# Where a layer-norm, lightning-attention and router kernel makes its second pair's token blocks and its softmax exponentials: from the heads stage to the v stage

## The chip, the cores and the metric

The kernel runs on one core of one Trainium2 chip. Times are device microseconds (us) of one execution, from its launch to its end; the number given for a kernel is the median of several executions. The kernel before takes 1105.56 us (median of 3, 1104.92 to 1107.88). A profile is one execution taken by the hardware profiler; its span runs from the first to the last instruction.

## The reference

The input `x` has 4 sequences of 512 tokens with 512 features, in float32. The core of what is computed:

```python
xn = layernorm(x)
# attention: the 4x512 tokens, 16 heads of 128, blocks of tokens with a decay
qkv = silu(einsum('bnf,of->bno', xn, w_qkv))            # q, k, v per head
o_inter = einsum(qi * q_decay, kv)                      # state of the blocks before
o_intra = einsum(einsum(qi, ki) * diag_decay, vi)       # inside a block
kv = block_decay * kv + einsum(ki * k_decay, vi)
out = norm_w * out * rsqrt(mean(out * out) + 1e-6)      # over all heads of a token
gate = sigmoid(einsum('bnf,of->bno', xn, w_gate))
s = einsum('bno,fo->bnf', gate * out, w_out)
# router
scores = softmax(xn @ router_weight.T + router_bias)    # 64 experts
topk_w, topk_idx = top_k(scores, 8)
g = silu(xn * sum(topk_w) + einsum(topk_w, expert_bias[topk_idx]))
return x + s * g
```

## The kernel before, in words

**Tiling.** The 4 sequences are two pairs (`PB` = 2); a sequence is `NT` = 4 tiles of 128 tokens, and 512 features are `FC` = 4 chunks of 128, in two halves of `KC` = 2. A product in float32 is made of three matmuls on operands that are split into a high part in the format fp32r and the rest (`PASSES`, L27). The high part is a cast by ScalarE (`split_hi`, L99), the low part a subtraction by VectorE or GpSimd (`split_lo`, L102).

**Seven products for eight.** The two sequences of a pair and the two halves of the features make a 2x2 block matrix of tokens; two groups of output features and the two halves make one of weights. `unit` (L495) multiplies them with seven block products (`PRODUCTS`, L39) in place of eight. The token blocks are B11, B21, B22 and four sums T1 to T4 (`token_sums`, L265), the weight blocks A11, A12, A22 and four sums S1 to S4. Each product is 6 matmuls of 128x128 by 128x512. `unit` puts them in 3 of the 4 banks of the PSUM pool `ps_mm`; VectorE adds the banks together (`add`, L503, row L504). After product number i, `unit` runs the functions in `after[i]`: these are the side steps in which all other work of the kernel is placed. `plain_unit` (L536) is the same with eight plain products.

**What sets the order.** The order is written by hand. Every engine works through its own instructions in the order in which the program issues them, and waits at the first whose input or buffer is not ready. Nearly all DMAs are issued by one engine, SyncE (SP), in program order too. A pool's buffer is used again when its last reader is done.

**The stages,** with their starts in the profiled execution:

1. *Start* (0 to 14.2 us). Loads; 24 transposes of the identity that keep TensorE busy (`warm_up(WARM)`, L146); the decay masks of the 16 heads, made by ScalarE and GpSimd and stored (`make_decays`, L168, `mask_decays`, L174); layer norm of the first tiles (`layer_norms`, L225: statistics on VectorE, and `rstd` by a power on GpSimd, one instruction for each sequence; `normalise_x`, L239); transposes of the tile (`transpose`, L246, into `xf`); its blocks (`plain`, L291, or with token sums `combine`, L277); the router's logits (`logits`, L328).
2. *v* (14.2 to 201.2 us): 16 units (loop at L926). The blocks of a tile have 128 columns in a slot that both pairs share in turn (`blocks[1, n] = blocks[0, n]`, L898). Units 0 to 3 are pair 0's tiles and units 4 to 7 pair 1's, with the first half of v's weights (`ws[0]`); while unit k runs, the side steps prepare tile k+1. Units 8 to 11 are pair 1's tiles again and 12 to 15 pair 0's, with the second half (`ws[1]`, loaded in unit 4, L945, its sums in units 4 to 7, L949). Since pair 1's blocks have then overwritten pair 0's, these are made again during units 9 to 12 from `xf`, which `turn` had stored in DRAM and `load_xf` (L295) loads. Four results of a unit go through tiles of `vout` (3 buffers, L877) to DRAM (`v_unit`, L587).
3. *Heads*: 24 units for pair 0 (from 201.2 us) and 24 for pair 1 (from 556.3 us), in the loop at L1004: a gate unit for two heads, then one qk unit for each. The attention of a head runs in the side steps of the unit behind its qk unit (`attention`, L732): `scores_qk`, `states` and `attend` for both sequences, and the second sequence's `attend` in step 0 of one unit later still. Scores, states and transposes use the pool `ps_sc` (3 PSUM banks), both outputs the one bank of `ps_o` (L712), which VectorE (`y`, L721) and ScalarE (`sq`, L728) read.
   Two more things run beside pair 0's heads. `rebuild` (L300, called at L1020) makes pair 1's blocks again from stored `xf`: in units 3, 7, 11 and 15, for one tile each, VectorE makes 4 token sums and 7 low parts and ScalarE 7 casts, and each block is stored to `blocks_d` (28 stores). At pair 0's end `load_block` (L201) loads them. `routing` (L345) runs one step after each product from unit 3 on: it loads the stored logits (`load`), takes the maximum and subtracts it (`top`, `less`), applies exponentials on ScalarE (`exps`), sums and divides (`total`, `norm`), takes the best 8 (`best_of`) and writes the weights' high and low parts transposed to DRAM (`turn`, with a bank of `ps_sc`).
4. *Output projection* (903.6 us to the end; `o_head`, L810, `finish`, L803), with the router's sums (`ffn`, L767).

Two of these orders, the attention of a head and the products of a unit on one tile, are these lines:

```python
now = [
    [], f(scores_qk, b1), f(scores_qk, b0), f(states, b1), f(states, b0), f(attend, b1), [],
]
return now, f(attend, b0)
...
return blocks[p, xn][:, xi, c, bass.ts(t, P)], w.of[wn][:, wi, bass.ts(c, VW)]   # v
return w.of[wn][:, wi, bass.ts(c, P)], blocks[p, xn][:, xi, c]                   # heads
```

Of the kernel before, what the change touches and what calls it, by code (L numbers as in the profile page):

```python
# [14 lines left out]
P = 128  # L15
# [7 lines left out]
WARM = 24  # L23
# [27 lines left out]
def kernel(  # L51
# [50 lines left out]
    def split_lo(eng, lo, src, hi):  # L102
# [22 lines left out]
    xf_d = {  # L125
        (p, t): dram.tile([P, PB, FC, P], F32, tag=f"xf{p}_{t}", name=f"xfd_{p}_{t}")
        for p in range(B // PB) for t in range(NT)
    }
# [3 lines left out]
        n: dram.tile([P, 2, KC, N], F32, tag=f"b{n}", name=f"bd_{n}") for _, n, _, _ in PRODUCTS  # L132
# [52 lines left out]
    rstd = [const.tile([P, NT], F32, tag=f"rstd{b}", name=f"rstd{b}") for b in range(B)]  # L185
# [11 lines left out]
    def block(p, i, xpool, slot):  # L197
        n = XN[i]
        blocks[p, n] = xpool.tile([P, 2, KC, N], F32R, tag=f"x{slot}", name=f"blk_{n}_{p}")
# [25 lines left out]
    def layer_norms(bs, t):  # L225
        var = small.tile([P, len(bs)], F32, tag="lnvar", name=f"lnv_{bs[0]}_{t}")
        for i, b in enumerate(bs):
# [4 lines left out]
                var[:, i : i + 1], stats[b][:, t, 1:2], 1.0, LN_EPS, ALU.mult, ALU.add  # L232
            )
        for i, b in enumerate(bs):
            nc.gpsimd.tensor_tensor(
                rstd[b][:, t : t + 1], var[:, i : i + 1], mhalf[:, 0:1], ALU.pow
            )
# [20 lines left out]
    def split_blocks(p, t, eng, srcs):  # L258
        for n, src in srcs:
            blk = blocks[p, n][:, :, :, bass.ts(t, P)]  # L260
            split_hi(blk[:, 0], src)
            split_lo(eng, blk[:, 1], src, blk[:, 0])
# [32 lines left out]
    def load_xf(stage, p, t):  # L295
        xfs[p, t] = stage.tile([P, PB, FC, P], F32, tag="xf", name=f"xf_again_{p}_{t}", bufs=2)
        nc.sync.dma_start(out=xfs[p, t], in_=xf_d[p, t])


    def rebuild(stage, p, t):  # L300
        def first():
            s = stage.tile([P, 4, KC, P], F32, tag="ts", name=f"ts_{p}_{t}_r", bufs=1)
            made.extend(token_sums(nc.vector, xfs[p, t], s))

        def lo(n, w):
            split_lo(nc.vector, w[:, 1], made[1][n], w[:, 0])
            nc.sync.dma_start(out=blocks_d[n][:, :, :, bass.ts(t, P)], in_=w.bitcast(F32))

        def step(i):
            if i == 0:  # L310
                first()
            if i > 0:
                lo(*done[-1])
            if i == len(XN):
                return
            n = XN[i]
            subs, src = made
            for f in {0: subs[0:2], 2: subs[2:4]}.get(i, ()):
                f()
            w = stage.tile([P, 2, KC, P], F32R, tag="piece", name=f"piece_{n}_{p}_{t}", bufs=3)  # L320
            split_hi(w[:, 0], src[n])
            done.append((n, w))

        made, done = [], []
        return [lambda i=i: step(i) for i in range(len(XN) + 1)]


    def logits(stage, p, t):  # L328
# [11 lines left out]
        if t == NT - 1:  # L340
            for j in range(PB):
                nc.sync.dma_start(out=scores_d[p * PB + j], in_=scores[p][:, j])


    def routing(stage):  # L345
# [7 lines left out]

        def top(b):
            den[b] = small.tile([P, NT], F32, tag="top", name=f"top_{b}")
            nc.vector.reduce_max(den[b], sc[b], axis=AX.X)

        def less(b):
            nc.vector.tensor_tensor(sc[b], sc[b], full(den[b]), ALU.subtract)

        def exps():
            for b in range(B):
                nc.scalar.activation(sc[b], sc[b], AF.Exp)
# [41 lines left out]
        for b in range(B):  # L405
            out += [lambda b=b: top(b), lambda b=b: less(b)]
# [498 lines left out]
    for i in range(2):  # L905
        ds[i] = make_decays(ds[i], hs[i])
# [257 lines left out]
```

## Time and profile before

| | us |
|---|---|
| median of 3 executions | 1105.56 (1104.92 to 1107.88) |
| the profiled execution, its time | 1105.03 |
| the profiled execution, its span | 1103.3 |
| mean granted TensorE clock | 0.992 of full |

| stretch of the span (us) | length | TensorE busy | VectorE | ScalarE | GpSimd | granted clock | DMA share |
|---|---|---|---|---|---|---|---|
| 0 to 20 (start) | 20 | 15.7 | 9.9 | 14.6 | 9.8 | 0.74 | 0.84 |
| 20 to 140 (v, tiles prepared) | 120 | 111.7 | 91.5 | 58.9 | 98.6 | 1.00 | 0.48 |
| 140 to 200 (v, rest) | 60 | 60.0 | 40.8 | 26.2 | 33.4 | 1.00 | 0.42 |
| 200 to 556 (heads, pair 0) | 356 | 345.2 | 251.6 | 171.8 | 259.1 | 0.99 | 0.44 |
| 556 to 900 (heads, pair 1) | 344 | 344.0 | 204.6 | 158.3 | 252.8 | 1.00 | 0.30 |
| 900 to 1098 (output) | 198 | 195.3 | 111.8 | 58.4 | 73.1 | 1.00 | 0.46 |

How the profile is read. Engines are called PE (TensorE's matmuls), PEld (its loads of the stationary operand, which overlap the matmuls), DVE (VectorE), ACT (ScalarE), POOL (GpSimd) and SP (SyncE). A row names the line of the kernel, the engine, the operation and `out<-in` by the program's names. A wait "A <- B" is idle time of A's engine that ended when B was done; where a wait has several conditions, it is put down to the one that came last. Matmuls are pipelined and their ends are modelled, so a rate is read from one start to the next. The granted clock is the share of full speed that the chip's throttle gave TensorE. DMA share is the mean busy share of 16 DMA engines. Some matmul records can be missing (a few per cent).

### The profile page before, as it was taken

To read this page: it belongs to the slowest core of one execution; us is meant where nothing else is said; L and a number is where in the kernel's file an instruction comes from. 1 tells how busy PE (TensorE), PEld (TensorE's weight loads), DVE (VectorE), ACT (ScalarE), POOL (GpSimd) and SP (SyncE) were. 2 spreads that over 40 slices of the span, in tenths; PEclk is the share of its full clock that TensorE was granted. 3 is DMA by queue.
4 is the path that set the end of the run, shared out by engine and by line. 5 is a ranking of instruction groups with operands and counts; after the bars stand their busy time and mean duration, and the time that the engine had idled before them with its cause. 6 is when DMAs were issued, how large, how long until landed. Compare 5 with 4: busy or idle time off the path is not lost.

```text
span 1103.3 us, 16497 instructions
## 1 busy us (share of the span) xinstructions
PE 1072.5 (97%) x5748; PEld 913.6 (83%) x5748; DVE 711.8 (65%) x1100; ACT 488.2 (44%) x966; POOL 726.8 (66%) x733
## 2 busy tenths in 40 slices
PE   8998999998989899999999999999999999999998
PEld 7787788787878788888888888888888888788886
DVE  5786876578686957756556556566565575855554
ACT  6454453455444444444444444444444443422311
POOL 6787883776666677767868677777778656722130
PEclk8999999999999999999999999999999999999999
DMA  7554342544343344444553222322422337354341
GB/s 235 192 180 184 114 172 111 185 129 138 101 139 130 110 143 128 122 125 154 185 195 93 86 76 91 107 82 81 125 82 81 97 104 244 129 183 152 125 168 61
DMA packets 116962, 147.27 MB, mean 133 GB/s; under 512 B 9232, under 2 KB 67728, under 8 KB 115984
## 3 DMA queue, kind: packets, MB, share of 16 engines
q1 hardware_dynamic: 116016, 145.52, 40.4%
q8 instruction: 45, 0.74, 0.3%
q10 hardware_dynamic: 864, 0.70, 0.2%
q14 instruction: 37, 0.30, 0.1%
HBM read 93.24 MB, written 52.95 MB: 133 GB/s over the span
## 4 chain that ended last, share of the span: by engine, by line
PE 75%; DVE 8%; issue 5%; POOL 4%; DMA 4%; ACT 3%; SPq 0%; DVEq 0%; ACTq 0%; POOLq 0%
PE u_qk L513 24%; PE po L812 13%; PE u_g L513 12%; PE u_v L513 6%; PE o L717 5%; PE sa L680 5%; PE o L719 3%; PE ss L703 3%; PE kt L683 2%; DMA yin<-y 1%; DMA v<-vo_v 1%; DVE ts_r L267 1%; DVE k L567 1%; DVE y L721 1%; POOL ts L267 1%
## 5 line engine op out<-in xcount | busy, mean ns | idle before, releaser
L812 PE MATMUL po<-wr,yr 128*128 128x512 f32 x768 | 179.8, 391 | 2.0 <-DVE u L806 1.6
L812 PEld LDWEIGHTS po<-wr,yr 128*128 128x128 f32 x768 | 143.6, 188 | 33.6 <-ACT yr L100 2.0
L513 PE MATMUL u_qk<-blk_T,ws_qk 128*128 128x512 f32 x576 | 150.3, 400 | 0.0
L729 POOL TENSOR_TENSOR sqs<-sqs,sq 128x512 f32<-128x512 f32 x60 | 77.2, 1287 | 92.1 <-ACT sq L728 87.8
L513 PEld LDWEIGHTS u_qk<-blk_T,ws_qk 128*128 128x128 f32 x576 | 104.9, 189 | 20.9
L707 DVE SCALAR_TENSOR_TENSOR st<-st,bdecay,ss 128x128 f32<-128x128 f32 x128 | 44.4, 348 | 99.4 <-ACT st L705 97.1
L513 PE MATMUL u_qk<-blk_B,wa_qk 128*128 128x512 f32 x384 | 101.2, 399 | 0.0
L103 POOL TENSOR_TENSOR ws_qk<-sum_qk,ws_qk 128x512 fp32r<-128x512 f32 x64 | 87.8, 1382 | 18.8 <-ACT ws_qk L100 18.8
L103 DVE TENSOR_TENSOR yr<-yin,yr 128x512 fp32r<-128x512 f32 x64 | 68.4, 1104 | 47.2 <-ACT yr L100 46.0
L717 PE MATMUL o<-at,vin 128*128 128x128 f32 x512 | 89.4, 277 | 4.9 <-ACT sq L728 4.8
L717 PEld LDWEIGHTS o<-at,vin 128*128 128x128 f32 x512 | 77.3, 192 | 12.1 <-ACT sq L728 7.1
L513 PEld LDWEIGHTS u_qk<-blk_B,wa_qk 128*128 128x128 f32 x384 | 71.5, 190 | 15.5
L513 PE MATMUL u_g<-blk_T,ws_g 128*128 128x512 f32 x288 | 79.2, 411 | 0.0
L689 ACT ACTIVATE kd<-kt,kdecay 128x384 f32<-128x384 f32 x64 | 37.3, 582 | 90.2 <-PE kt L683 90.2
L719 PE MATMUL o<-qd,st 128*128 128x128 f32 x384 | 74.8, 277 | 0.0
L680 PEld LDWEIGHTS sa<-q,k 128*128 128x128 f32 x512 | 66.7, 191 | 8.1 <-DVE q L567 2.2
L721 DVE SCALAR_TENSOR_TENSOR y<-o,nw,gt 128x512 f32<-128x512 f32 x64 | 47.9, 748 | 36.9 <-PE o L719 35.5
L564 ACT ACTIVATE sg_k<-k 128x512 f32<-128x512 f32 x64 | 40.5, 632 | 69.5 <-DVE k L504 69.5
L680 PE MATMUL sa<-q,k 128*128 128x128 f32 x512 | 67.7, 275 | 1.7 <-DVE q L567 1.5
L776 POOL TENSOR_TENSOR u<-u,sgu 128x512 f32<-128x512 f32 x16 | 20.7, 1292 | 73.4 <-ACT sgu L775 58.2
L513 PE MATMUL u_v<-w_S_v,blk_T 128*128 128x512 f32 x252 | 63.1, 393 | 3.9 <-DVE a_v L504 2.1
L691 POOL TENSOR_TENSOR qd<-q,dec 128x384 f32<-128x384 f32 x64 | 66.4, 1039 | 0.0
(188 smaller groups left out, 2478.1 us busy)
## 6 DMA issues: line engine op xcount, KB each, us to landing
v<-vo_v SPq DMA_DIRECT2D x64, 256.0 KB, 2.0
raw_qk<-in_w_head_dram SPq DMA_DIRECT2D x64, 256.0 KB, 4.5
vin<-v SPq DMA_DIRECT2D x64, 256.0 KB, 3.6
y<-y SPq DMA_DIRECT2D x64, 256.0 KB, 2.1
yin<-y SPq DMA_DIRECT2D x64, 256.0 KB, 3.2
x<-in_x_dram SPq DMA_DIRECT2D x32, 256.0 KB, 4.9
raw_g<-in_w_head_dram SPq DMA_DIRECT2D x32, 256.0 KB, 2.9
raw_v<-in_w_v_dram SPq DMA_DIRECT2D x16, 256.0 KB, 4.6
```

Source lines behind the costliest of these rows:

```text
L103: eng.tensor_tensor(lo, src, hi.bitcast(F32), ALU.subtract)
L513: nc.tensor.matmul(ps, lhsT, rhs, start=(first and c == 0 and n == 0), stop=(c == KC - 1 and n == len(PASSES) - 1), skip_group_check=not f ...
L564: nc.scalar.activation(sg, src, AF.Sigmoid)
L680: nc.tensor.matmul(pa[:, c], k[:, c], q[:, c], start=True, stop=True)
L689: nc.scalar.activation(kd[s], pk, AF.Copy, scale=kdecay[:, h : h + 1])
L691: nc.gpsimd.tensor_tensor(qd[s], q[:, 1:], d[:, 1, None, :].to_broadcast([P, NT - 1, P]), ALU.mult)
L707: nc.vector.scalar_tensor_tensor(r[:, c], r[:, c - 1], bdecay[:, h : h + 1], ps[:, c], ALU.mult, ALU.add)
L717: nc.tensor.matmul(o, v_of(b, h, c), at[s][:, c], start=True, stop=(c == 0))
L719: nc.tensor.matmul(o, st[s][:, c - 1], qd[s][:, c - 1], start=False, stop=True)
L721: nc.vector.scalar_tensor_tensor(y, po, nw[:, h : h + 1], gts[s], ALU.mult, ALU.mult)
L729: nc.gpsimd.tensor_tensor(sq[b], sq[b], s1, ALU.add)
L812: nc.tensor.matmul(pos[t], yr[:, yi, bass.ts(t, P)], wos[h][:, wi], start=(h == 0 and n == 0), stop=(h == NH - 1 and n == len(PASSES) - 1),)
```

## The change

- **Pair 1's blocks.** Blocks are laid out by tile, `[P, NT, 2, KC, P]` instead of `[P, 2, KC, N]`, in SBUF and in DRAM. In the four v units of pair 1's tiles, `keep_blocks` stores the unit's tile of all seven blocks after the last product (28 stores of 256 KB). `rebuild`, its loads of `xf` and pair 1's stores of `xf` are gone. The heads now read a block's 512 columns as 4 runs of 128.
- **Softmax.** The maximum and its subtraction run in v units 5 and 6 for pair 0 and 10 and 11 for pair 1, on both sequences at once; the exponentials of both pairs run in unit 13, and the four stores of the scores follow them. `routing` begins with the sum. `logits` stores nothing.
- **Outputs.** The second sequence's `attend` takes a bank of `ps_sc` instead of `ps_o`.
- **v.** `vout` has 4 buffers instead of 3; two sums of `ws[1]` run after product 3 instead of 5.
- **Start.** 32 warm-up transposes instead of 24, and 6 more ahead of the first blocks and logits. Only the first 4 heads' decays come ahead of the first normalisation, the other 12 behind the second tile's; the cast of A11 comes ahead of the first transposes. A tile's two `rstd` come from one instruction of GpSimd.

```diff
-WARM = 24
+WARM = 32
...
-    xf_d = {
-        (p, t): dram.tile([P, PB, FC, P], F32, tag=f"xf{p}_{t}", name=f"xfd_{p}_{t}")
-        for p in range(B // PB) for t in range(NT)
-    }
+    xf_d = [dram.tile([P, PB, FC, P], F32, tag=f"xf{t}", name=f"xfd_{t}") for t in range(NT)]
...
-        n: dram.tile([P, 2, KC, N], F32, tag=f"b{n}", name=f"bd_{n}") for _, n, _, _ in PRODUCTS
+        n: dram.tile([P, NT, 2, KC, P], F32, tag=f"b{n}", name=f"bd_{n}") for _, n, _, _ in PRODUCTS
...
-    rstd = [const.tile([P, NT], F32, tag=f"rstd{b}", name=f"rstd{b}") for b in range(B)]
+    rstd_of = [const.tile([P, NT, PB], F32, tag=f"rstd{p}", name=f"rstd{p}") for p in range(B // PB)]
+    rstd = [rstd_of[b // PB][:, :, b % PB] for b in range(B)]
...
-        blocks[p, n] = xpool.tile([P, 2, KC, N], F32R, tag=f"x{slot}", name=f"blk_{n}_{p}")
+        blocks[p, n] = xpool.tile([P, NT, 2, KC, P], F32R, tag=f"x{slot}", name=f"blk_{n}_{p}")
...
-        for i, b in enumerate(bs):
-            nc.gpsimd.tensor_tensor(
-                rstd[b][:, t : t + 1], var[:, i : i + 1], mhalf[:, 0:1], ALU.pow
-            )
+        nc.gpsimd.tensor_tensor(rstd_of[p][:, t], var, mhalf[:, 0:PB], ALU.pow)
...
-            blk = blocks[p, n][:, :, :, bass.ts(t, P)]
+            blk = blocks[p, n][:, t]
...
-    def rebuild(stage, p, t):
...
+    def keep_blocks(p, t):
+        for n in XN:
+            nc.sync.dma_start(out=blocks_d[n][:, t], in_=blocks[p, n].bitcast(F32)[:, t])
...
-        if t == NT - 1:
-            for j in range(PB):
-                nc.sync.dma_start(out=scores_d[p * PB + j], in_=scores[p][:, j])
+    def scores_less(p, what):
+        sc = scores[p].rearrange("p b t e -> p (b t) e")
+        if what == "top":
+            scores[p, "top"] = small.tile([P, PB * NT], F32, tag="top", name=f"top_{p}", bufs=2)
+            nc.vector.reduce_max(scores[p, "top"], sc, axis=AX.X)
+        else:
+            top = scores[p, "top"][:, :, None].to_broadcast([P, PB * NT, E])
+            nc.vector.tensor_tensor(sc, sc, top, ALU.subtract)
+
+    def scores_exp():
+        for p in range(B // PB):
+            nc.scalar.activation(scores[p], scores[p], AF.Exp)
+        for b in range(B):
+            nc.sync.dma_start(out=scores_d[b], in_=scores[b // PB][:, b % PB])
...
         out = [load]
-        for b in range(B):
-            out += [lambda b=b: top(b), lambda b=b: less(b)]
-        out.append(exps)
...
-            return blocks[p, xn][:, xi, c, bass.ts(t, P)], w.of[wn][:, wi, bass.ts(c, VW)]
+            return blocks[p, xn][:, t, xi, c], w.of[wn][:, wi, bass.ts(c, VW)]
...
-            return w.of[wn][:, wi, bass.ts(c, P)], blocks[p, xn][:, xi, c]
+            return w.of[wn][:, wi, bass.ts(c, P)], blocks[p, xn][:, :, xi, c]
...
-        return now, f(attend, b0)
+        return now, [lambda: attend(b0, h, attp, (ps_sc, "sc"))]
...
-            nc.sync.dma_start(out=xf_d[p, t], in_=xfs[p, t])
+            if p == 0:
+                nc.sync.dma_start(out=xf_d[t], in_=xfs[p, t])
...
-    vwp, vout = left(vw_stack, "vw", 8), left(vw_stack, "vout", 3)
+    vwp, vout = left(vw_stack, "vw", 8), left(vw_stack, "vout", 4)
...
-    for i in range(2):
-        ds[i] = make_decays(ds[i], hs[i])
+    ds[0] = make_decays(ds[0], hs[0])
     prep[0]["stats"]()
     prep[0]["norms"]()
+    ws[0].split_one("A11", nc.vector)
     prep[0]["turn"]()
     load_pair(stage, *tiles[2])
-    for i in range(2):
-        mask_decays(ds[i], hs[i])
-    ws[0].split_one("A11", nc.vector)
+    mask_decays(ds[0], hs[0])
+    warm_up(6)
     prep[0]["sums"]()
     ws[0].split_one("A12", nc.gpsimd)
     prep[0]["logits"]()
     prep[1]["stats"]()
     prep[1]["norms"]()
-    for i in range(2, 4):
+    for i in range(1, 4):
         ds[i] = make_decays(ds[i], hs[i])
     ws[0].split_one("A21", nc.vector)
     ws[0].split_one("A22", nc.gpsimd)
-    for i in range(2, 4):
+    for i in range(1, 4):
         mask_decays(ds[i], hs[i])
 
     for k, (p, t) in enumerate(tiles + again):
         g, after = k // n1, nothing()
+        for unit_of, what in ((n1 - 3, (0, "top")), (n1 - 2, (0, "less")), (n1 + 2, (1, "top")), (n1 + 3, (1, "less"))):
+            if k == unit_of:
+                after[2].append(lambda what=what: scores_less(*what))
+        if n1 - NT <= k < n1:
+            after[6].append(lambda p=p, t=t: keep_blocks(p, t))
...
-            after[0 if n == 3 else 5].append(lambda n=n, eng=eng: ws[1].sum_of(n, eng))
+            after[0 if n == 3 else 5 if n == 2 else 3].append(lambda n=n, eng=eng: ws[1].sum_of(n, eng))
...
+        if k == n1 + NT + 1:
+            after[1].append(scores_exp)
...
-        t, step = divmod(i - 2, 4)
-        if 0 <= t < NT:
-            if step == 0:
-                load_xf(again, 1, t)
-                again_steps = rebuild(again, 1, t)
-            if step == 1:
-                for j in range(len(PRODUCTS)):
-                    after[j].append(again_steps.pop(0))
-            if step == 2:
-                after[0].append(again_steps.pop(0))
```

More of the change, by code (lines that the diff above doesn't have):

```diff
@@ L223, in load_x, with layer_norms @@
         xts[b, t] = xt
-    def layer_norms(bs, t):
-        var = small.tile([P, len(bs)], F32, tag="lnvar", name=f"lnv_{bs[0]}_{t}")
-        for i, b in enumerate(bs):
+    def layer_norms(p, t):
+        var = small.tile([P, PB], F32, tag="lnvar", name=f"lnv_{p}_{t}")
+        for j in range(PB):
+            b = p * PB + j
             st = small.tile([P, nc.vector.BN_STATS_DIM], F32, tag="bn", name=f"bn_{b}_{t}")
@@ L231, in layer_norms @@
             nc.vector.tensor_scalar(
-                var[:, i : i + 1], stats[b][:, t, 1:2], 1.0, LN_EPS, ALU.mult, ALU.add
+                var[:, j : j + 1], stats[b][:, t, 1:2], 1.0, LN_EPS, ALU.mult, ALU.add
             )
-        for i, b in enumerate(bs):
-            nc.gpsimd.tensor_tensor(
-                rstd[b][:, t : t + 1], var[:, i : i + 1], mhalf[:, 0:1], ALU.pow
-            )
+        nc.gpsimd.tensor_tensor(rstd_of[p][:, t], var, mhalf[:, 0:PB], ALU.pow)
     def normalise_x(bs, t):
@@ L293, in plain, with load_xf @@
         split_blocks(p, t, eng, (("B11", b11), ("T1", b12), ("B21", b21), ("B22", b22)))
-    def load_xf(stage, p, t):
+    def load_xf(stage, t):
+        p = 0
         xfs[p, t] = stage.tile([P, PB, FC, P], F32, tag="xf", name=f"xf_again_{p}_{t}", bufs=2)
-        nc.sync.dma_start(out=xfs[p, t], in_=xf_d[p, t])
-    def rebuild(stage, p, t):
[L301 to L325, printed above, removed]
+        nc.sync.dma_start(out=xfs[p, t], in_=xf_d[t])
+    def keep_blocks(p, t):
+        for n in XN:
+            nc.sync.dma_start(out=blocks_d[n][:, t], in_=blocks[p, n].bitcast(F32)[:, t])
     def logits(stage, p, t):
@@ L352, in load @@
                 nc.sync.dma_start(out=sc[b], in_=scores_d[b])
[L354 to L361, printed above, removed]
-            for b in range(B):
-                nc.scalar.activation(sc[b], sc[b], AF.Exp)
         def total(b):
@@ L404, in routing @@
         out = [load]
-        for b in range(B):
-            out += [lambda b=b: top(b), lambda b=b: less(b)]
-        out.append(exps)
         for b in range(B):
@@ L837, in prepare @@
         return {
-            "stats": lambda: layer_norms(bs, t), "norms": lambda: normalise_x(bs, t),
+            "stats": lambda: layer_norms(p, t), "norms": lambda: normalise_x(bs, t),
             "turn": turn, "sums": sums[0], "more": sums[1], "logits": route_logits,
@@ L957 @@
         if n1 <= k < n1 + NT:
-            after[0].append(lambda t=t: load_xf(stage, 0, t))
+            after[0].append(lambda t=t: load_xf(stage, t))
         if n1 < k <= n1 + NT:
```

## The prediction

> **What bounds the kernel now.** First the page: the share of busy time says TensorE, so the only time to win is the time in which TensorE stands still or runs slowly.
>
> ```profile
> PE 1072.5 (97%) x5748; PEld 913.6 (83%) x5748; DVE 711.8 (65%) x1100; ACT 488.2 (44%) x966; POOL 726.8 (66%) x733
> ```
>
> Then the windows of 20 us, to see where. From 140 to 200 and from 460 to 900 TensorE is busy in all 20 us of nearly every window: nothing that other engines lose or gain there counts. It has holes at the start, from 40 to 140 (the v stage) and from 240 to 400 (pair 0's heads, where the rebuild of pair 1's blocks and the routing run beside attention). The waits of TensorE in 215 to 470 us (total, times, longest) name the last to arrive:
>
> ```profile
> PE o L717 <- ACT sq L728: 4.8, 3, 2.7
> PE u_qk L513 <- DVE k L504: 3.4, 2, 3.1
> PE sa L680 <- DVE q L567: 1.5, 1, 1.5
> PE sa L680 <- DVE k L567: 0.3, 1, 0.3
> ```
>
> Together 10.0 us. VectorE's rows before the longest show what "DVE k" (the sum that frees a PSUM bank) was queued behind (start, length):
>
> ```profile
> 308.87 0.72 DVE L103 TENSOR_TENSOR piece_T<-ts_r,piece_T 128x256 fp32r<-128x256 f32 x1
> 309.51 0.96 DVE L267 TENSOR_TENSOR ts_r<-xf_again 128x256 f32<-128x256 f32 x1
> 310.39 0.95 DVE L267 TENSOR_TENSOR ts_r<-xf_again,ts_r 128x256 f32<-128x256 f32 x1
> ...
> 311.73 1.03 DVE L103 TENSOR_TENSOR piece_T<-ts_r,piece_T 128x256 fp32r<-128x256 f32 x1
> 312.69 0.17 DVE L381 TENSOR_REDUCE sumw<-best 128x4 f32<-128x32 f32 x1
> 312.78 1.38 DVE L382 TENSOR_TENSOR scores_in<-scores_in,rest 128x256 f32<-128x256 f32 x1
> 314.09 0.68 DVE L504 TENSOR_TENSOR k<-u_qk,e_qk 128x512 f32<-128x512 f32 x1
> ```
>
> It waited behind rebuild (piece_T, ts_r) and routing, with VectorE never idle. A long hole costs twice: in the windows by stage (TensorE, loads, DVE, ACT, POOL, granted clock, DMA) a stretch with little TensorE work is followed by one at half clock.
>
> ```profile
> 311.60:315.00 3.40, 0.31 (x2) 0.18 (x2) 3.40 (x7) 0.20 (x1) 2.28 (x2) 1.00 0.31 88
> 315.00:318.40 3.40, 3.40 (x9) 2.63 (x10) 3.40 (x6) 2.47 (x6) 2.09 (x3) 0.50 0.29 77
> ```
>
> **Heads of pair 0.** Undisturbed units, by the starts of their first products, repeat as gate 16.68, odd qk 15.11, even qk 11.32 us (470.05, 486.73, 498.05, 513.16). Pair 0 has a first gate unit of 11.15 and a first qk unit of 9.80, then 8 odd, 7 gate and 7 even ones: 11.15 + 9.80 + 120.88 + 116.76 + 79.24 = 337.8. The routing's four turns add 4 x 0.44 = 1.8: 339.6. The trace has 556.27 - 201.22 = 355.05, so 15.5 us are lost: 10.0 of waits, two half-clock stretches (the second at 383) of 1.7 each, the rest restarts.
>
> The change takes away VectorE's 28 low parts (10.4 + 9.7 us, piece_T and piece_B), 16 token sums (7.2 + 6.5), 4 maxima (1.6) and 4 subtractions (2.4): 37.8 us; from ScalarE 28 casts (11.2), 4 exponentials (1.3) and two table loads (2.6): 15.1 us; from the queues four loads of 512 KB and 28 stores of 256 KB. In 365 to 385, VectorE was busy 18.99 of 20 us; eleven rebuild operations (33.8 / 4 = 8.4 us) leave it with 10.6. The `sq` waits end with the one PSUM bank of `ps_o`: `attend(b0)` now takes a bank of `ps_sc`. **What is late next:** in the three-bank ring the next head's second `sa` waits for that bank. It starts 4.1 us after the output's last product (287.4 to 291.50) and `sq` was done at 289.62, so 1.9 us are spare even in a disturbed unit. The routing's `total` still waits for `scores_in` (1.70 us idle of VectorE at 244.4); no TensorE wait follows there now. Turns move by some steps; each needs a third bank 2.4 us after an `sa` whose mask product ends about 1.2 after it: covered. I take 14 of 15.5; bounds 10 and 15.5.
>
> **The v stage.** Its units from 2 on take 14.5, 12.3, 12.2, 14.7, 13.8, 11.1, 11.3, 10.0 and then 9.52 us; a unit with transposes and logits costs 12.2 undisturbed, so about 10 us are lost. Of these, unit 5's 2.1 us is this: VectorE's row at 88.46 waits for a store, because `vout` has three buffers and four tiles a unit, and that store (issued 81.23, 7.11 us to landing in the chain) lies behind eight loads of 256 KB.
>
> ```profile
> 86.63 1.21 DVE L452 TENSOR_TENSOR sum_v<-raw_v 128x1024 f32<-128x1024 f32 x1
> 88.46 0.69 DVE L504 TENSOR_TENSOR vo_v<-u_v,a_v 128x512 f32<-128x512 f32 x1 [0.62 <-DMA v<-vo_v]
> ```
>
> The fourth buffer makes the wait one for a store a unit old, and the weight sum of 1.21 goes to an earlier step: 2.1 gone. The next wait (POOL blk_T, 1.3 at 101) goes back to it: POOL stood 6.1 us before 92.29 for `lnv`, which VectorE made late. Units 7 to 9 lose 3.9, mostly to weight splits that stay; I give 0.6 back. Unit 2's 2.3 stays. Sum 4; bounds 1 and 7. The joined `rstd` saves nothing: it starts with the second `lnv`, as its second half did.
>
> Added: 28 stores of 256 KB on SP, seven at the end of each of units 4 to 7. The eight loads took 5.27 us to issue (0.66 each), so seven take 4.6. Behind them stand that unit's last v store and, after unit 7, the next `xf` load. The store's buffer is wanted again some 10 us later, the bytes (1.8 MB) take 5 to 6 us at the 300 to 370 GB/s of the first 20 us: hidden. A late `xf` would delay POOL's sums at 131, but POOL then waits 3.80 us for ScalarE anyway. If that cover goes, each of four units loses up to unit 5's 2.1. The eight `xfd` and `scd` stores leave the queue; four `scd` stores return in unit 13. VectorE gets 2 maxima and 2 subtractions of 128x512 (0.8 each by two 128x256 ones), while it is idle 3 to 7 of each 20 us there.
>
> ScalarE gets in unit 13 two table loads (1.28 each) and two exponentials (0.67 each): 3.9 us in a stage where it is busy half the time. The sigmoid behind them comes some 1.1 us late; its bank is wanted 5 us later: 0. The Trainium skill ("ScalarE: Activation LUTs", rules for kernel authors) tells to budget about 2.7 us for a switch of sets (its own section on the load measured 1.28); the trace's row has 1.28. With the page's figure the block would be 6.7 us and the sigmoid 3.9 late, still inside the 5.
>
> **The start.** The warm-up ends about 0.9 us later (8 x 0.109), but the first transpose also comes later, since both normalisations wait for one `rstd` (x at 8.29 instead of 7.29). ScalarE's first weight cast moves from 11.05 to about 8.6, the four block splits end about 1.9 earlier. Half clock held from 7.8 to 18.0, after a stretch in which TensorE was busy 1.30 of 3.40 us; with 1.59 busy of 3.40 (at 254) the clock stayed. Eight more warm-ups make that stretch 2.2: if it stays up, the first v product starts near 12.7 instead of 14.15, but the second half then waits for A21 and A22, whose casts stand behind twelve decays (12 x 0.41) instead of eight, 0.8 us later. If it falls, the six extra warm-ups cost 0.9. Value 0.5; bounds -1 and 2.5. The Trainium skill ("TensorE: Matmul & The Clock Gate", part 1) has the fall after an idle window of about 3.4 us; the trace's fall came with 1.30 busy inside the window, so the rows decide; by the page this start would not have fallen at all and the eight would be worth nothing.
>
> **The place of the blocks.** Six v products in a row take 1.36 us, six of the heads 1.40, with the same shapes (next start minus start):
>
> ```profile
> 197.13 1.52 PE L513 MATMUL u_v<-w_S_v,blk_T 128*128 128x512 f32 x6
> 198.49 1.52 PE L513 MATMUL u_v<-w_S_v,blk_B 128*128 128x512 f32 x6
> ...
> 210.97 1.56 PE L513 MATMUL u_g<-blk_T,wb_g 128*128 128x512 f32 x6
> 212.37 1.56 PE L513 MATMUL u_qk<-blk_B,wa_qk 128*128 128x512 f32 x6
> ```
>
> So the rate depends on where or how operands are read (226.7 against 233.3 ns), and the change moves the blocks by 128 bytes and makes the heads read four runs of 128 columns 2 KB apart instead of one of 512. No row shows such a read. Bounds: all 2016 products at v's rate, -13.4 us; at the slow end one such difference (6.7 ns) more for each of three jumps, 2016 x 20 ns = +40. I take 0, the unchanged row, which is nearest in shape. The Trainium skill ("SBUF — State Buffer", the door on the DMA port swizzle) speaks of 16-byte lines and a penalty for crossings; runs of 512 bytes cross as many lines as before, which would leave the rate alone; no row here shows it.
>
> **Sum.** 14 + 4 + 0.5 = 18.5 off the profiled 1105.0 (span 1103.3 and 1.7 around it; median of runs 1105.6): **1086.5 us.**
>
> **Rivals.** (1) *The jumps cost* (slower): place, every product of 48 head units; price up to 40, so 1086.5 + 40 = 1127; from 18.5 us / 2016 = 9.2 ns a product, 3.1 a jump, it undoes the gain. For it: the rate does depend on the reading. Against: the two rates seen lie 6.7 ns apart, and 9.2 are needed. (2) *The blocks land well*: heads at v's rate for most products, some 10 us more: 1076. (3) *The stores collide*: the v gain is lost and four units lose 2.1: 1086.5 + 4 + 8.4 = 1099. For it: the 7.11 us landing; against: DMA share 0.32 to 0.36 in 100 to 140. (4) *The heads' stalls stay*: routing alone overloads VectorE or its wait for `scores_in` is handed on; half of 14 stays: 1093.5. Against: unit 15 rebuilt without routing and lost 0.2, so one of the two is bearable.
>
> **Numbers.** Forecast 0.60; (1) 0.08; (2) 0.14; (3) 0.12; (4) 0.06. The range 1074 to 1097 takes in the forecast's bounds (11 to 25 off, less likely together), (2) and (4) and the near part of (3). A measurement here tells 0.3% (3.3 us). Slower comes from (1) alone, whose mild end is near no change: faster 0.90, same 0.03, slower 0.07.
>
> **What would show it.** Right: no `o <- sq` and `u_qk <- DVE k` among TensorE's waits, no half clock after 20 us, pair 0's heads near 341 us, v units 5 and 6 near 12.3, no `vo <- DMA` wait. Wrong: head products not at 1.40 per six (place), v units 5 to 9 waiting for a store (collision), a new `sa <- sq` (the bank).

## The result, and the profile after

The changed kernel takes 1091.99 us (median of 4, 1089.88 to 1092.30) against 1106.38 for the kernel before (median of 4): a ratio of 0.9866 (95% interval 0.9846 to 0.9885), 14.4 us less. The prediction was 1086.5 with a range of 1074 to 1097. The profiled execution is the fastest of the four, 1089.88 us with a span of 1088.2; its stretches, read from the first v, head and output products, add up to the difference of the spans, 15.1 us:

| stretch | before | after | difference | predicted difference |
|---|---|---|---|---|
| start to v unit 2 | 44.06 | 46.50 | +2.44 | -0.5 |
| v units 2 to 15 | 157.16 | 158.94 | +1.78 | -4 |
| heads of pair 0 | 355.05 | 337.80 | -17.25 | -14 |
| heads of pair 1 | 347.32 | 345.25 | -2.07 | 0 |
| output and end | 199.70 | 199.67 | -0.03 | 0 |

So the heads gave more than was forecast, and the start and the v stage, which were to give 4.5 us together, lost 4.2. By the page, TensorE has 14 instructions more (the warm-ups), and VectorE is busy for 25 us less (711.8 before):

```profile
PE 1063.4 (98%) x5762; PEld 912.5 (84%) x5762; DVE 686.9 (63%) x1052; ACT 480.1 (44%) x936; POOL 723.0 (66%) x725
```

**Heads.** The waits of TensorE in 200 to 550 us (total, times, longest) were of five kinds and 10.8 us in the kernel before: the four shown in the prediction, 10.0 together, and 0.8 for a weight. Now there is one:

```profile
PE sa L654 <- DVE q L541: 1.6, 2, 0.9
```

No output waits for a square, no product for a bank that VectorE frees, and no stretch of half clock is left between 91 and 910 us. Undisturbed units are shorter too, in both pairs: pair 0's gate, odd and even units take 16.60, 14.98 and 11.15 us (16.68, 15.11 and 11.32 before). The rows of the products show why. Six of them take 1.36 us from start to start here, as six v products already did, where they took 1.40; on average a product of pair 0's heads takes 229.3 ns, where it took 232.6:

```profile
212.87 1.52 PE L487 MATMUL u_g<-blk_B,ws_g 128*128 128x512 f32 x6
214.23 1.52 PE L487 MATMUL u_g<-blk_T,wb_g 128*128 128x512 f32 x6
215.59 1.52 PE L487 MATMUL u_qk<-blk_B,wa_qk 128*128 128x512 f32 x6
```

**v.** Two units grew by more than 4 us, unit 1 from 14.46 to 18.69 and unit 4 from 12.23 to 17.03, and three (0, 2 and 7) by 0.15 to 0.33; units 5 and 6 fell from 14.67 and 13.82 to 13.13 and 12.26. In unit 4, these are VectorE's rows (start, length):

```profile
81.02 1.81 DVE L205 TENSOR_SCALAR x<-x,stats,rstd 128x512 f32<-128x512 f32 x2 [0.22 <-POOL rstd L233]
85.70 1.55 DVE L426 TENSOR_TENSOR sum_v<-raw_v 128x1024 f32<-128x1024 f32 x1 [2.87 <-DMA raw_v<-in_w_v_dram]
87.17 0.68 DVE L478 TENSOR_TENSOR vo_v<-u_v,e_v 128x512 f32<-128x512 f32 x1
```

The weight sum, moved from the step after product 5 to that after product 3, is at the head of VectorE's queue before its weights have landed: their eight loads are issued in the same unit, from 76.05 on. The sum that frees a PSUM bank (`vo_v`, 87.17) stands behind it, and TensorE, whose rows these are, behind that:

```profile
83.02 1.64 PE L487 MATMUL u_v<-w_S_v,blk_B 128*128 128x512 f32 x6
87.90 2.93 PE L487 MATMUL u_v<-w_A_v,blk_T 128*128 128x512 f32 x6 [3.25 <-DVE vo_v L478]
```

The hole is charged twice, as in the kernel before. In the windows by stage (TensorE, loads, DVE, ACT, POOL, granted clock, DMA share, GB/s), the stretch with 0.65 us of TensorE in 3.41 is followed by one at half clock:

```profile
80.59:84.01 3.42, 3.42 (x24) 3.11 (x24) 2.03 (x3) 0.17 (x1) 3.34 (x5) 1.00 0.89 285
84.01:87.42 3.41, 0.65 (x3) 0.19 (x1) 1.72 (x2) 0.00 (x0) 2.16 (x4) 1.00 0.84 311
87.42:90.84 3.42, 2.94 (x7) 2.36 (x8) 2.75 (x5) 2.38 (x6) 1.96 (x3) 0.50 0.21 77
```

**The start.** The clock now stays up from 5.5 to 32.8 us, and the first v product comes at 12.21 instead of 14.15. But unit 1 then stands still until VectorE frees its banks, and is fined with half clock as well. ScalarE's rows (first fence) and VectorE's (second) hold the chain, TensorE's (third) the hole, and the windows by stage (fourth) the half clock behind it:

```profile
12.90 4.91 ACT L168 ACTIVATE mkdecay<-dist,slopes 128x256 f32<-128x256 f32 x12
17.70 1.99 ACT L100 CAST w_A_v<-raw_v 128x1024 fp32r<-128x1024 f32 x2
19.59 1.06 ACT L249 COPY xf<-pt 128x512 f32<-128x512 f32 x2
20.67 1.28 ACT L538 ACT_TABLE_LOAD   x1
21.96 1.09 ACT L538 ACTIVATE sg_v<-d_v 128x512 f32<-128x512 f32 x2
```

```profile
22.59 0.69 DVE L541 TENSOR_TENSOR vo_v<-d_v,sg_v 128x512 f32<-128x512 f32 x1 [2.59 <-ACT sg_v L538]
...
26.12 1.80 DVE L205 TENSOR_SCALAR x<-x,stats,rstd 128x512 f32<-128x512 f32 x2 [0.82 <-POOL rstd L233]
27.85 1.75 DVE L426 TENSOR_TENSOR sum_v<-raw_v 128x1024 f32<-128x1024 f32 x1
30.71 1.23 DVE L103 TENSOR_TENSOR w_S_v<-sum_v,w_S_v 128x1024 fp32r<-128x1024 f32 x1 [1.11 <-ACT w_S_v L100]
31.85 1.28 DVE L541 TENSOR_TENSOR vo_v<-d_v,sg_v 128x512 f32<-128x512 f32 x2
```

```profile
27.81 1.64 PE L519 MATMUL d_v<-w_A_v,blk_B 128*128 128x512 f32 x6
32.68 2.78 PE L519 MATMUL d_v<-w_A_v,blk_T 128*128 128x512 f32 x6 [3.23 <-DVE vo_v L541]
```

```profile
29.40:32.81 3.41, 0.18 (x2) 0.16 (x2) 2.30 (x4) 1.70 (x3) 0.79 (x1) 1.00 0.98 306
32.81:36.22 3.41, 3.41 (x11) 2.73 (x12) 2.25 (x4) 1.49 (x2) 0.60 (x1) 0.50 0.60 229
```

In the kernel before, `vo_v` came at 22.46 and 30.98, the first normalisation did not wait for the second sequence's `rstd`, and TensorE's wait was 0.58 us:

```profile
25.08 0.54 DVE L207 TENSOR_SCALAR x<-x,stats,rstd 128x512 f32<-128x512 f32 x1
26.06 0.95 DVE L207 TENSOR_SCALAR x<-x,stats,rstd 128x512 f32<-128x512 f32 x1 [0.45 <-POOL rstd L235]
...
30.98 1.28 DVE L567 TENSOR_TENSOR vo_v<-d_v,sg_v 128x512 f32<-128x512 f32 x2
```

```profile
31.81 1.62 PE L545 MATMUL d_v<-w_A_v,blk_T 128*128 128x512 f32 x6 [0.58 <-DVE vo_v L567]
```

Twelve decays on ScalarE kept its chain where it was, although TensorE was 1.9 us ahead, and the two normalisations at 26.12, which now wait for one `rstd` together, made VectorE 0.9 later.

### The profile page after: what moved, and what is told of

Same layout as the page of the kernel before. It is cut to its first block, busy times and chain, and to the rows that moved or that the text cites. A ratio compares the mean times of both kernels' runs of the same rounds, so it can differ in the third digit from the quotient of the medians.

```text
span 1088.2 us, 16459 instructions
## 1 busy us (share of the span) xinstructions
PE 1063.4 (98%) x5762; PEld 912.5 (84%) x5762; DVE 686.9 (63%) x1052; ACT 480.1 (44%) x936; POOL 723.0 (66%) x725
## 4 chain that ended last, share of the span: by engine, by line
PE 87%; DVE 5%; ACT 2%; issue 2%; POOL 1%; DMA 1%; SPq 1%; DVEq 0%; ACTq 0%; POOLq 0%
PE u_qk L487 27%; PE po L786 16%; PE u_g L487 14%; PE u_v L487 9%; PE sa L654 5%; PE o L691 5%; PE ss L677 4%; PE o L693 4%; PE kt L657 2%; DMA raw_v<-in_w_v_dram 1%; DVE vo_v L541 1%; PE pu L746 1%; PE lg L308 0%; DVE vo_v L478 0%; ACT w_A_v L100 0%
```

## The experiments

Differences of a stretch are read from its first products in one profiled execution each; medians are of 4 or more executions. Average times of a product are from start to start, with gaps of 260 ns and more left out. The reading of a v unit is disturbed by the half clock, which comes once, twice or not at all after the same hole (last section).

**e1: the weight sum back behind product 5.**

```diff
-            after[0 if n == 3 else 5 if n == 2 else 3].append(...sum_of...)
+            after[0 if n == 3 else 3 if n == 1 else 5].append(...sum_of...)
```

> The changed kernel with one edit: the first weight sum of v's second half (unit 4) stands after product 5 again, as before; the second one (unit 5) stays after product 3. Theory A: unit 4 takes 17.03 us in the changed kernel because this sum, moved two products ahead, waits on VectorE for weights that were only asked for in the same unit (2.87 us idle, landing at 85.70), with the bank sum of product 4 queued behind it; TensorE stands 3.25 us and then gets 3.4 us of half clock (1.7 lost). Put back, unit 4 takes 12.3 and the half clock at 87.4 is gone: 4.8 us faster than the changed kernel (1085.1 by the profiled run's 1089.9). Rival B: the weights land late in either place, and the wait only moves to unit 5's banks: unit 5 grows from 13.1 to 15 or more, and less than 2.5 us are won.

Unit 4 took 12.27 us (17.03), unit 5 13.28 (13.13), and there was no half clock between 39 and 906 us. Median 1086.15 (1083.46 to 1087.98; ratio to the kernel before 0.9815, 0.9795 to 0.9835), 5.8 us under the changed kernel. Theory A holds; B's price in unit 5 was 0.15. VectorE's row of the sum, at its old place, has no wait for the weights:

```profile
87.81 1.57 DVE L426 TENSOR_TENSOR sum_v<-raw_v 128x1024 f32<-128x1024 f32 x1
```

In this execution unit 1 met two stretches of half clock and took 19.99 us (18.69), so that unit 2 started at 48.16; v units 2 to 15 took 154.34, 2.8 us less than in the kernel before.

**e2: the old start.**

```diff
-WARM = 32
+WARM = 24
...
-    ds[0] = make_decays(ds[0], hs[0])
+    for i in range(2):
+        ds[i] = make_decays(ds[i], hs[i])
...
-    ws[0].split_one("A11", nc.vector)
     prep[0]["turn"]()
...
-    mask_decays(ds[0], hs[0])
-    warm_up(6)
+    for i in range(2):
+        mask_decays(ds[i], hs[i])
+    ws[0].split_one("A11", nc.vector)
...
-    for i in range(1, 4):
+    for i in range(2, 4):
         ds[i] = make_decays(ds[i], hs[i])
...
-    for i in range(1, 4):
+    for i in range(2, 4):
         mask_decays(ds[i], hs[i])
```

> The changed kernel with the start's order as before: 24 warm-up transposes and no six later ones, 8 decays ahead of the first normalisation and 8 behind the second, the cast of A11 behind the first transposes. The joined rstd stays. Theory A: the new start brings TensorE to its first v product 1.9 us earlier (12.21 against 14.15), but VectorE, tied to a power on GpSimd that stands behind 12 masks instead of 8, frees the banks of unit 1 no earlier, so that TensorE stands 3.2 us at 29.5 and then gets half clock at 32.8 to 36.2; unit 2 starts at 46.50 against 44.06. With the old start unit 2 starts near 44.1 and the time falls by 2.4 us. Rival B: the hole in unit 1 comes from the joined rstd (two normalisations together, 0.9 us later) or from v's stores, which stay here: then unit 1 keeps its wait and the time rises by 1.9 us, the lost gain of the start.

The first v product came at 13.94 and unit 2 at 44.73, 1.8 us earlier than in the changed kernel: the new start loses, as A says. But A wanted 44.1. Unit 1 took 15.21 us where the kernel before takes 14.46, and the joined `rstd` is what of the change is left there: rows of VectorE have both normalisations at 25.93, where the kernel before did one at 25.08 and the other at 26.06. So B has 0.75 us of it. How much the new start loses hangs on the half clock behind unit 1's hole: with it once, unit 2 starts at 46.38 to 46.63 (e4, e6, e11), but in e5 and e7, which have the same start and no half clock there, at 44.93 and 44.85, hardly later than here. The median, 1091.25, is only 0.7 lower; in the profiled execution, two stretches of half clock followed unit 4's hole (units 4 and 5 took 18.10 and 14.61 us, 17.03 and 13.13 in the changed kernel).

**e3: fewer warm-ups,** `WARM` = 24 and no `warm_up(6)`, the rest of the new start kept.

> The changed kernel with 24 warm-up transposes instead of 32 and without the six later ones; the rest of the new start stays. Theory A: the extra warm-ups keep the clock up (full until 32.8 in the changed kernel, half from 4.5 to 8 on until 18 with 24), but unit 1's banks are freed by the chain ScalarE (12 decays, casts, table load, sigmoid) and VectorE, whose times do not follow TensorE's clock. So the first v product comes 1.5 us later or more, and unit 2 still starts between 44.5 and 46.5, as with 32. Rival B: TensorE's clock sets the start, and unit 2 starts 1.5 us later than in the changed kernel (46.50), at 48.

The clock was at half from 9.70 to 16.53, the first v product came at 13.86, and unit 2 at 46.58 (46.50). Median 1092.63 against 1091.99. Theory A: the warm-ups win 1.65 us for TensorE, and units 0 and 1 take them back to the tenth (one stretch of half clock in unit 1 in both).

**e4: the second sequence's output in the one bank of `ps_o`.**

```diff
-        return now, [lambda: attend(b0, h, attp, (ps_sc, "sc"))]
+        return now, f(attend, b0)
```

> The changed kernel, with the second sequence's output back in the one bank of ps_o. Theory A: with the rebuild's 28 casts and the exponentials gone from ScalarE, the squares that free that bank come early enough by themselves: pair 0's heads (337.8 us) grow by less than 1 us, and the part of the 13 us won that belongs to the bank is nearly nothing. Rival B: the bank was the cause of the 4.8 us of waits of an output on a square; they come back, 3 to 5 us in pair 0's heads.

Pair 0's heads took 338.93 us (+1.1), pair 1's 345.70 (+0.4); median 1092.65 (+0.7). No wait of an output on a square came back. Theory A, with 1.1 us for the second bank, just over the 1 that was named: with ScalarE's lighter load those waits end without it. That the bank alone would not have ended them does not follow; e7 has the bank and the old load, and no such wait either.

**e5: softmax back in the heads,** with `top`, `less` and `exps` as in the kernel before, and plain stores in unit 13.

> The changed kernel, but softmax's maxima, subtractions and exponentials stand in pair 0's heads again (4.0 us of VectorE, 1.3 us of exponentials and 2.6 us of table loads on ScalarE, 9 steps ahead of the sums); the scores are stored in v's unit 13 as they are. Theory A: without the rebuild beside it this is bearable: pair 0's heads grow from 337.8 by 0.5 to 2 us, v does not move. Rival B: routing alone makes VectorE late: 4 us or more. Rival C: v gets faster by 0.5 us or more because unit 13 loses its table loads and units 5, 6, 10 and 11 their steps.

Pair 0's heads took 338.80 us (+1.0). The new small tiles shift the blocks by 64 bytes, which made head products 0.6 ns longer (229.85 against 229.27, 0.6 us in 1008 products), so softmax alone is worth some 0.4 us. Units 13, 10 and 11 did not move (9.52); unit 7 took 0.7 more (12.19), with a longer wait for a bank sum whose cause was not followed. Theory A, at its lower end. Median 1092.97.

**e6: the rebuild back in the heads,** with its loads and stores, and without the 28 stores in v.

```diff
+        t, step = divmod(i - 2, 4)
+        if 0 <= t < NT:
+            if step == 0:
+                load_xf(again, 1, t)
+                again_steps = rebuild(again, 1, t)
...
-            after[6].append(lambda p=p, t=t: keep_blocks(p, t))
```

> The changed kernel, but pair 1's blocks are rebuilt in pair 0's heads as before (28 low parts and 16 sums on VectorE, 28 casts on ScalarE, stores of xf and its loads) and the 28 stores of v units 4 to 7 are gone; the layout by tile, the early exponentials and the second bank stay. Theory A: the rebuild alone made most of the 13 us of stalls; pair 0's heads grow from 337.8 to 345 to 350 us, and v's units 4 to 7 stay as they are (the stores were hidden). Rival B: rebuild was bearable without the softmax steps beside it, and with a bank of ps_sc for the output: heads grow by less than 3 us. Rival C: the 28 stores cost v 1 us or more, which comes back in units 5 to 8.

Pair 0's heads took 345.00 us (+7.2); v units 6 to 8, which follow the stores closest, 12.26, 11.47 and 11.30 (12.26, 11.47 and 11.32 with them). Median 1096.72 (+4.7). Theory A against B, and C is out: the 28 stores are hidden. The 7.2 has one stretch of half clock in it (322 us, up to 1.7), and this execution was the slowest of its four (1100.03).

**e7: both back in the heads.**

> The changed kernel with both put back into pair 0's heads, the rebuild and the softmax; layout, second bank and start stay as changed. Rebuild alone cost 7.2 us in pair 0's heads. Theory A: the two cost more together than apart, since they share VectorE in the same steps: pair 0's heads come to 349 to 351 (11 to 13 us over 337.8), of 355.05 before; the rest of the difference is the place of the blocks (about 3 us) and the bank (about 1). Rival B: they add: rebuild's 7.2 and the 0.5 to 2 of softmax alone, 345.5 to 347, so that some 4 us more of before's loss belong to something else, the one bank above all.

Pair 0's heads took 352.28 us, 14.5 more than in the changed kernel, of which 0.6 is the shift of 64 bytes. Apart, the two cost 7.2 and 0.4, together 13.9: some 6 us belong to neither alone, of which up to 3.4 are two more stretches of half clock than in e6 (273, 317 and 389 us). The waits of TensorE in 200 to 550 us, of e6 (first) and e7 (second), show it. The wait for the bank that VectorE frees (`k`) has grown from 0.6 to 3.7:

```profile
PE sa L684 <- DVE q L571: 3.6, 3, 2.3
PE u_qk L517 <- DVE a_qk L508: 0.6, 1, 0.6
PE u_qk L517 <- DVE k L508: 0.6, 1, 0.6
```

```profile
PE sa L696 <- DVE q L583: 5.2, 2, 2.6
PE u_qk L529 <- DVE k L520: 3.7, 2, 3.2
PE sa L696 <- DVE k L583: 0.4, 1, 0.4
```

No wait of an output on a square is among them, although ScalarE has its old load (169.9 us busy in pair 0's heads, 170.7 in the kernel before): here the second bank is enough to end those waits. But the time came back at `sa` (5.2 us; 1.7 in e8, which has the one bank and the old load). B's four missing microseconds do not exist: the 2.8 us between 352.28 and the 355.05 of before are the place of the blocks (232.56 against 229.88 ns, 2.7 us in 1008 products). The median is 1105.93 (ratio 1.0007, 0.9995 to 1.0020): without the lighter heads, the rest of the change wins no more than it loses.

**e8: the kernel before, with the blocks moved by 128 bytes.**

```diff
+    gap = pool(ctx, "gap").tile([P, 32], F32, tag="gap", name="gap")
+    nc.gpsimd.memset(gap, 0.0)
     xa = pool(ctx, "xa")
```

> The kernel before with 128 more bytes per partition set aside ahead of the blocks, and nothing else (one small fill on GpSimd at the start). The blocks then lie 0 instead of 128 bytes from the head weights, modulo 512. Theory A: the place sets the rate: in the kernel before, products of heads take 232.6 ns from start to start where stationary and moving operand lie 128 bytes apart modulo 512, and 230.1 where they lie 0 apart (pair 1's four slots on the other side); 232.9 and 226.9 in the output projection. So 1008 products of pair 0 gain 2.5 ns each, 432 of pair 1 too, 140 to 190 of the output 6: 4.4 us in all, and a rate near 230.1 for all heads. Rival B: the rate is one of the layout or of the pool, not of the address: no change, 232.6 in pair 0.

Products of the heads took 229.33 and 229.53 ns on average (232.56 and 231.19), those of the output 226.89 (228.06). Pair 0's heads took 350.72 us (-4.3) and pair 1's 345.60 (-1.7), and undisturbed units 16.60, 14.99 and 11.15, those of the changed kernel to 0.01. Of the 4.3, 1008 products at 3.2 ns are 3.3; the second stretch of half clock, at 383 us in the kernel before, did not come here. Here are the products (start, length) with the blocks in their old layout:

```profile
209.99 1.52 PE L515 MATMUL u_g<-blk_T,wb_g 128*128 128x512 f32 x6
211.35 1.52 PE L515 MATMUL u_qk<-blk_B,wa_qk 128*128 128x512 f32 x6
```

Median 1100.42 against 1105.85 in the same runs (ratio 0.9957, 0.9943 to 0.9972): 5.4 us for 128 unused bytes. Theory A.

**e9: the changed kernel, with the same 128 bytes.**

> The changed kernel with the same 128 bytes set aside ahead of the blocks; they then lie 384 instead of 256 bytes from the head weights, modulo 512. In the changed kernel all head products take 229.3 to 229.6 ns, at a distance of 256 as at 0. Theory A: a distance that is an odd multiple of 128 costs, whatever the layout: pair 0's products go to 232.6 (3.3 us more), the 432 of pair 1 on that side too (1.4 us), and those of the output on that side to 232.9 (0.8 us): 5.5 us slower than the changed kernel. Rival B: reading four runs of 128 columns is what is faster, and the address does nothing: no change, 229.3. Rival C: only 128 costs, 384 does not: no change either, told from B by the kernel before with the same bytes.

Products of pair 0 took 232.56 ns and pair 1's 231.19, to the hundredth what they take in the kernel before; pair 0's heads 340.31 us (+2.5), pair 1's 346.98 (+1.7). Median 1095.49 (+3.5). The rows:

```profile
215.76 1.56 PE L489 MATMUL u_g<-blk_T,wb_g 128*128 128x512 f32 x6
217.16 1.56 PE L489 MATMUL u_qk<-blk_B,wa_qk 128*128 128x512 f32 x6
```

A and not B: the four runs of 128 columns cost nothing and win nothing, the place does it. The distance from block to head weights, worked out from the tiles' addresses, is 128 bytes modulo 512 here, as in the kernel before; the expectation's 384 had the sign wrong, so that A and C were not told apart.

**e10: e1, with 8 of the 16 decays made in v's units 12 and 14.**

```diff
+    def late_decays(i):
+        d = make_decays(decay_space(i), hs[i])
+        mask_decays(d, hs[i])
...
-    for i in range(1, 4):
+    for i in range(1, 2):
         ds[i] = make_decays(ds[i], hs[i])
...
+        if k in (n1 + NT, n1 + NT + 2):
+            after[1].append(lambda i=2 if k == n1 + NT else 3: late_decays(i))
```

> The kernel e1 (weight sum after product 5) with a start that has only 8 decays: those of heads 8 to 15 are made in v's units 12 and 14 (each with four exponentials, two table loads, four masks, four stores), where ScalarE was busy half the time. Theory A: ScalarE's 12 decays behind the second tile's norm (4.9 us) set the first sigmoid (21.96), VectorE's first bank sum (22.59) and so the 3.2 us hole in unit 1; with 8 fewer (3.3 us) that chain comes about 1.5 us earlier, the hole shrinks to 1.7 or less, its half clock (1.7 to 3.4 us lost) mostly goes, and unit 2 starts at 42 to 44 instead of 46.5 to 48; units 12 to 15 stay at 9.5. Time 1081 to 1084. Rival B: the power on GpSimd or VectorE's order sets the hole: unit 2 at 46 or later. Rival C: units 12 and 14 lose 1 us or more each to ScalarE.

The first sigmoid came at 20.89 (21.96) and unit 1's hole was 1.3 us (3.2), with no half clock before 903 us:

```profile
28.68 1.64 PE L519 MATMUL d_v<-w_A_v,blk_B 128*128 128x512 f32 x6
31.63 0.70 PE L519 MATMUL d_v<-w_A_v,blk_T 128*128 128x512 f32 x2 [1.31 <-DVE vo_v L541]
```

Unit 2 started at 43.84 (48.16 in e1, with two stretches of half clock; 44.85 and 44.93 in e7 and e5, with none), units 12 to 15 stayed at 9.52. Median 1083.62 (ratio 0.9790, 0.9774 to 0.9806). Theory A; the chain moved by 1.07 us rather than 1.5, since the second normalisation on VectorE came next.

**e11: e1 with 3 buffers for `vout`.**

> The kernel e1 with vout back at 3 buffers. Theory A: the fourth buffer won what the prediction said, a wait of VectorE for a store that lies behind eight loads: unit 5 (13.28 us in e1) grows by 1 to 2.1 us, and v's units 6 to 8 by up to 0.5 each, now that 7 stores of blocks stand in the queue too. Rival B: that wait went with the weight sum's move to another step: under 0.5 us in all.

Unit 5 took 15.77 us (13.28 in e1), unit 11 10.81 (9.52), and the first gate unit behind v 11.66 (9.98): 5.5 us, of which the medians, 1090.31 and 1086.15, show 4.2. VectorE's waits in 60 to 210 us, and one of its rows ahead of the heads:

```profile
DVE vo_v L478 <- DMA v<-vo_v: 7.3, 11, 2.7
```

```profile
204.00 0.69 DVE L478 TENSOR_TENSOR vo_v<-u_v,a_v 128x512 f32<-128x512 f32 x1 [0.56 <-DMA v<-vo_v]
```

Theory A, at more than its price: e1 has no wait of that kind.

**e12: e10, with each sequence's `rstd` from an instruction of its own.**

```diff
-        nc.gpsimd.tensor_tensor(rstd_of[p][:, t], var, mhalf[:, 0:PB], ALU.pow)
+        for j in range(PB):
+            nc.gpsimd.tensor_tensor(
+                rstd_of[p][:, t, j : j + 1], var[:, j : j + 1], mhalf[:, 0:1], ALU.pow
+            )
```

> The kernel e10 with each sequence's rstd from its own instruction again. Theory A: the joined rstd makes the first normalisation wait for both sequences' statistics; in unit 1 (old start, joined against single) that was 0.75 us of VectorE, 15.21 against 14.46 us. Where VectorE still sets the end of unit 1, 0.5 to 1 us come back; elsewhere nothing moves. Time 0.5 to 1 us under e10. Rival B: unit 1's hole is closed in e10 already or set by ScalarE, and the two agree within 0.3 us; GpSimd's one more instruction a tile costs nothing either way.

Unit 1 took 14.39 us (15.15 in e10) and unit 2 started at 42.85 (43.84); what is left of TensorE's waits in 30 to 200 us on VectorE's bank sums of unit 1 is 0.5:

```profile
PE u_v L490 <- DVE a_v L481: 2.3, 2, 1.4
PE u_v L490 <- POOL blk_B L103: 1.1, 1, 1.1
PE u_v L490 <- DVE vo_v L481: 0.9, 2, 0.5
PE d_v L522 <- DVE vo_v L544: 0.5, 1, 0.5
```

Median 1081.84 (1080.62 to 1082.86; ratio to the kernel before 0.9774, 0.9757 to 0.9791), 1.8 under e10 where 0.5 to 1 was expected. It beats both kernels.

## Why the prediction was right, and where it was wrong

The time lies in the range and the sign is right, but 18.5 us were forecast and 14.4 measured, and two errors of the sum stand against one that helped. That it came so near is in part luck: with the place of the blocks as before, which the forecast took, the gain is 10.4 us (1105.85 - 1095.49, e9), just inside the bounds. Their lower ends, 10, 1 and -1, add up to 10 and not to the 11 that the prediction names.

- **Heads' stalls, 14: right.** With the place of the blocks held as before, the difference is 355.05 - 340.31 = 14.7 us (e9); with the place as after, 350.72 - 337.80 = 12.9 (e8). That rebuild and routing overload VectorE together, while one of the two is bearable, was rival 4's counter-argument, and e5 to e7 bear it out (0.4, 7.2, 13.9, half clock included), though 7.2 is not little. On the square's waits, bank or lighter load is each enough to end them (e7, e4); the bank, which the prediction named, was worth 1.1 us here.
- **v, 4: wrong, and in its sign.** Unit 5's wait for a store went, and units 5 and 6 won 1.5 and 1.6. The fourth buffer is worth more than the 2.1 (5.5 between e1 and e11; that it also covers the block stores there is likely, not shown). The step that failed is "the weight sum of 1.21 goes to an earlier step: 2.1 gone". It counted what the sum leaves behind, and never asked whether its weights have landed two products earlier; they had not, and unit 4 lost 4.8 us (e1). No rival had it. Without that step the term was right in sign, and 2.8 for 4 in size (e1).
- **The start, 0.5 with bounds -1 and 2.5: wrong, +2.4 us.** The prediction saw that the clock might stay up and that twelve decays would delay ScalarE, and priced it in unit 0, at 0.8 us. The bill came in unit 1, with 3.2 us of waiting and a stretch of half clock on top; where that stretch did not come, the start and units 0 and 1 lost 0.8 to 0.9 (e7, e5). "The joined `rstd` saves nothing" held only half of it: the joined `rstd` costs 0.75 us (e2, e12). Saving the clock was worth nothing (e3), because ScalarE and VectorE set that stretch. That eight more warm-ups keep it up was right: the window behind the first rise had 1.73 us of TensorE's work (2.2 was forecast) and the clock stayed, with 24 it had 1.20 and 1.24 and the clock fell (e3, e2). The 1.59 us at 254 were cut off the clock's grid; on it (253.58 to 256.99) they are 1.95.
- **The block stores hidden: right** (e6). Rival 3 named v units 4 to 8; unit 4 did lose, but its wait was for a load and not for a store.
- **The softmax in unit 13 at 0: right**; unit 13 stayed at 9.52, and the two table loads took 1.28 us each.
- **Place, 0 between -13.4 and +40: mis-sized.** It measured -4.2 to -6.1 us in the heads of both pairs (e9, e8). Rival 1 is out, jumps cost nothing (229.33 ns without, e8, and 229.27 with). Rival 2 was right in its mechanism at half its price. About a third of the change's gain (4.2 to 6.1 of 15.1 us) thus comes from the 128 bytes by which the blocks were moved. The Trainium skill ("SBUF — State Buffer", the door on the DMA port swizzle) has a penalty for each access that crosses to a new 16-byte line; that the runs of 512 bytes, which cross no more lines, cost nothing agrees with it. What moved the rate is the place (e8, e9).

## What to carry to other kernels

A step that is moved forward has to be checked against the landing of its operands as much as against what stands behind it on its engine: here one weight sum, two products early, cost 4.8 us. Before speeding up the engine that bounds, follow the chain of the other engines to the next bank that they free, since time won ahead of it was handed back here, and with half clock. By the traces here, a hole of less than about 1.8 us costs its own length alone (an estimate, last section), a longer one may cost up to 1.7 or 3.4 us on top. And when a change alters any tile's size, compare the start-to-start time of unchanged products in the two traces before crediting the change: an empty tile of 128 bytes, alone in the kernel before, gave 5.4 us.

## What the runs showed of the hardware

- **Where operands lie.** Products of 128x128 by 128x512 in fp32r take 232.6 ns in the heads where stationary and moving operand lie 128 bytes apart modulo 512, and 229.3 to 230.6 where they lie 0, 192 or 256 apart; in the output projection 232.9 to 233.3 against 226.8 to 227.3 at 0 or 256, and 229.1 to 229.3 at 192. (The distances are worked out from the tiles' addresses.) That the address alone does it is shown (e8, e9). For the distance, and against the moving operand's own place, speaks the kernel before: with the moving operand at 352 modulo 512, products take 227.2 ns in v, where the stationary one lies at 352 too, and 232.6 and 232.9 in heads and output, where it lies at 480. Why is open, and 384 wasn't tried.
- **Half clock comes in steps of 3.41 us on a grid of its own.** The first full-clock stretch starts between 4.3 and 7.4 us from one execution to another, and every later change lies a multiple of 3.41 us behind it, but for some 10 ns. So one and the same hole in unit 1 meets the grid differently: 17.07 and 17.09 us with no stretch of half clock (e5, e7), 18.38 to 18.71 with one (after, e4, e6, e11), 19.78 and 19.99 with two (e9, e1); each costs up to 1.7 us (half of 3.41). It is likely, and not shown, that executions of the changed kernel differ by 2 us in part for this reason. The Trainium skill ("TensorE: Matmul & The Clock Gate", part 1) says that the window is free-running and 3413 ns long, and the traces agree. It has the fall after an idle window, while here it also came after windows with 0.65 us (84.01) and 1.30 us (4.4, before) of TensorE's work; the measurement decides.
- **How little work makes the clock fall.** All 14 traces were cut on this grid, and the one-column sums `ssq` left out of TensorE's work (16 of them, 2 us of busy time by the profile, stand at the start of pair 1's heads and 16 at that of the output projection). Then the windows at full clock fall into two: each of the 39 with at most 1.43 us of work was followed by half clock, and none of the 4354 with 1.54 us or more. So a single hole of less than about 1.8 us (an estimate: 3.41 - 1.54) should not be followed by half clock, wherever it falls; e10's hole of 1.31 was not.
